# A list scheduler with new durations, a price on changes of TensorE's tiling and ScalarE's table, and new places

## The chip, the cores and the metric

The kernel runs on one core of one Trainium2 chip. A core has five engines that run their own queues of instructions: TensorE (PE in the profile, its weight loads PEld), VectorE (DVE), ScalarE (ACT), GpSimd (POOL) and SyncE (SP, which here only issues DMA transfers). The metric is the device time of one execution in microseconds (us), less is better; the median of three runs is given.

## The reference

The input `x` has 2 batches of 2048 tokens with 128 features. Four layers are added to it one after the other, each on the layer norm of its input, all in float32:

```python
x = x + attn_a(layernorm(x))    # softmax(x x^T, axis=1) x: full attention, 2048 x 2048 per batch
x = x + ffn(layernorm(x))       # two layers, see below
x = x + attn_b(layernorm(x))    # a weight per token, a weight per channel, one projection
x = x + ffn(layernorm(x))       # the same two layers and weights again

def layer(x, ...):              # one of the two layers of ffn
    h = shift_token(x)                       # half the features come from the token before
    q, k, v = split(h @ wqkv)                # 8 heads of 64
    q, k = rotary_xpos(l2norm(q) * qs, l2norm(k) * ks)
    x = x + local_attention(q, k, v) @ wo    # windows of 64, each sees itself and the one before
    h = layernorm(shift_token(x)) * lg + lb
    a, g = split(h @ w1 + b1)                # 341 each
    return x + (a * gelu(g)) @ w2 + b2
```

## The kernel before

The state is held with features on the 128 partitions (`xT`, 128 x 4096). A batch is cut into 16 blocks of 128 tokens and 4 chunks of 512.

**What one block does** (`Attention.block`, a layer's attention for 128 tokens). `project` (L584) makes queries and keys as two operations of 16 matmuls with 32 output rows each, placed in the four column strips of the array (`tile_position=(0, c * 32)`), and L591 the values with the whole array. ACT copies the values (L592) and squares the projections (L607); DVE multiplies them with the rotary tables (L608, L609) and sums the squares (L612); one whole-array matmul adds the halves (L613); ACT and POOL make the inverse root (L617, L618, `newton` L394 to L397); POOL adds the rotated halves and scales (L616, L622); DVE turns queries and keys by 32 x 32 blocks (L631, L632). `scores` (L654, with the mask added by L663) is one operation of 74 matmuls on 64 x 32 tiles. DVE takes the maximum (L675), ACT eight exponentials (L680), DVE sum and reciprocal (L686, L687), POOL scales (L692), DVE turns (L703). Four DMA writes to DRAM (L712) and one read back (L717) set the turned weights out for `combine` (L728): 32 matmuls of 64 output rows. ACT copies (L735), and every second block `out_proj` (L741) multiplies with `wo` and DVE adds it to the state (L747, L748).

**Feed-forward**, per chunk of 512: `center` (L504 to L509) makes mean and inverse root with whole-array matmuls, POOL scales (L773 in the profile), six matmul operations with `w1` (L777), of which the three gate products fill three PSUM banks until `gelus` (L785) has read them; DVE multiplies (L793), `down` (L802) multiplies with `w2`.

**Stages.** The first attention of batch 0 stands alone at the start (`first_attention`, L453 to L468). Then the program is written down tick by tick, 71 ticks: two layers of one batch run 6 ticks apart, the four passes (two batches, twice) follow each other 16 ticks apart and overlap by 7. The first attention of batch 1 (`second_attention`, L484 to L497) is spread over the first 16 ticks; its tiles `e` serve as work tiles `w` of the blocks once it is over. `token_weights` (L861 to L984) is the third layer.

**What sets the order.** None of this is the order on the engines. Each call of `op` only records an operation with its engine, a cost in us, its reads and writes, the tiles that it claims, and `late`. `Program.run` then plays the five engines forward in time with these costs: whenever an engine is free, it takes of its ready operations the one with the smallest key (its number in the program plus `late`) for which tiles are to be had, among the next `AHEAD = 600` operations. A block has some 45 operations. `TAIL` is the time from an operation's end until another engine sees it, `TABLE = 1.3` what ACT pays for another activation table (`act="E"` for exponential and logarithm, `"G"` gelu, `"S"` sigmoid). The order that comes out is the order of every queue; it is fixed when the kernel is built. Tiles come from pools (`slots`): 8 PSUM banks (`p1`), work tiles `w`, chunks `c` and others.

## Time and profile before

| | |
|---|---|
| Runs | 1557.29, 1552.46, 1549.56 us; median 1552.46 |
| Profiled execution | span 1551.6 us from first to last instruction; no time outside it is given |
| PE busy | 1456.4 us (94%), 20331 matmuls |
| DVE busy | 1337.8 us (86%) |
| POOL busy | 1071.3 us (69%) |
| ACT busy | 961.8 us (62%), of it 91.1 us in 71 table loads of 1283 ns in the table of groups, 72 in the whole trace |
| PE clock granted | 0.981 on the mean, 0.88 from 600 to 700 us, 0.86 behind 1500 us |
| DMA | 213.64 MB, engines 48.2% busy for the kernel's own queue |

PE in the profile counts a matmul from its start to its modelled end; matmuls are pipelined, so pieces of PE overlap. A 512-column product in float32 stands as two matmuls. Pieces of the chain of work that ended last give a start, a length and what worked; `x16` is the number of matmuls. A line of the waits gives who waited for whom, the total in us, how often, and the longest.

### The profile page before, as it was taken

To read this page: it belongs to the slowest core of one execution; us is meant where nothing else is said; L and a number is where in the kernel's file an instruction comes from. 1 tells how busy PE (TensorE), PEld (TensorE's weight loads), DVE (VectorE), ACT (ScalarE), POOL (GpSimd) and SP (SyncE) were. 2 spreads that over 40 slices of the span, in tenths; PEclk is the share of its full clock that TensorE was granted. 3 is DMA by queue.
4 is the path that set the end of the run, shared out by engine and by line. 5 is a ranking of instruction groups with operands and counts; after the bars stand their busy time and mean duration, and the time that the engine had idled before them with its cause. 6 is when DMAs were issued, how large, how long until landed. Compare 5 with 4: busy or idle time off the path is not lost.

```text
span 1551.6 us, 50597 instructions
## 1 busy us (share of the span) xinstructions
PE 1456.4 (94%) x20331; PEld 817.6 (53%) x20331; DVE 1337.8 (86%) x2468; ACT 961.8 (62%) x2449; POOL 1071.3 (69%) x1308
## 2 busy tenths in 40 slices
PE   7999999999999998899999999899999999999876
PEld 3455455555555554545555555545555555555443
DVE  4277866988899999979989999989999999998881
ACT  6446655666567766557656656576767676666661
POOL 4446434676598859649777869568787878895671
PEclk9999999999999999989999999899999999999998
DMA  7441442454465444535555654445646555647432
GB/s 236 147 150 45 120 113 66 117 165 117 121 167 138 139 110 113 161 106 139 154 140 141 174 135 113 105 126 161 176 136 195 161 140 164 183 139 208 125 90 71
DMA packets 204653, 213.64 MB, mean 138 GB/s; under 512 B 39594, under 2 KB 164996, under 8 KB 204420
## 3 DMA queue, kind: packets, MB, share of 16 engines
q1 hardware_dynamic: 204420, 210.43, 48.2%
q8 instruction: 160, 2.62, 0.7%
q14 instruction: 73, 0.60, 0.1%
HBM read 111.78 MB, written 61.87 MB: 112 GB/s over the span
## 4 chain that ended last, share of the span: by engine, by line
PE 56%; DVE 28%; POOL 5%; DMA 4%; issue 3%; ACT 3%; SPq 0%; POOLq 0%; DVEq 0%; ACTq 0%
PE pp L584 8%; PE pp L777 7%; PE pp L728 5%; PE pp L741 5%; PE pp L654 4%; PE pp L591 4%; PE pp L484 4%; PE pp L494 4%; PE pp L468 4%; PE pp L802 3%; DVE b_n L612 3%; DVE arena L609 2%; DVE b_m L675 2%; PE pp L460 2%; DVE b_m L686 2%
## 5 line engine op out<-in xcount | busy, mean ns | idle before, releaser
L584 PE MATMUL pp<-wqkv,b_s 128*32 128x256 f32 x4096 | 256.7, 386 | 4.8 <-DVE b_s L811 3.0
L680 ACT ACTIVATE arena<-pp,b_m 128x96 f32<-128x96 f32 x656 | 162.8, 362 | 78.3 <-DVE b_m L675 63.9
L692 POOL TENSOR_TENSOR arena<-arena,b_m 128x384 f32<-128x384 f32 x164 | 132.5, 826 | 110.6 <-DVE b_m L687 67.9
L777 PE MATMUL pp<-b_c,w 128*128 128x512 f32 (+1 forms) x384 | 181.7, 616 | 12.0 <-POOL b_c L773 8.9
L584 PEld LDWEIGHTS pp<-wqkv,b_s 128*32 128x32 f32 x4096 | 118.0, 110 | 132.6 <-issue 31.7
L607 ACT ACTIVATE arena<-pp 128x512 f32<-128x512 f32 x166 | 99.3, 618 | 82.1 <-PE pp L584 70.3
L622 POOL TENSOR_TENSOR arena<-arena,b_n 128x1024 f32<-128x1024 f32 x75 | 143.4, 1914 | 2.7
L675 DVE TENSOR_REDUCE b_m<-pp 128x4 f32<-128x384 f32 x256 | 131.0, 540 | 14.4 <-PE pp L663 13.5
L654 PEld LDWEIGHTS pp<-kring,b_c 64*32 64x32 f32 x8448 | 105.0, 106 | 70.9 <-issue 21.6
L654 PE MATMUL pp<-kring,b_c 64*32 64x96 f32 (+2 forms) x8448 | 132.8, 249 | 9.3 <-DVE kring L632 6.5
L591 PE MATMUL pp<-wqkv,b_s 128*128 128x512 f32 x256 | 138.8, 627 | 0.6 <-ACT b_c L508 0.6
L777 PEld LDWEIGHTS pp<-b_c,w 128*128 128x128 f32 (+1 forms) x384 | 66.4, 182 | 99.0 <-issue 66.0
L592 ACT COPY b_v<-pp 128x512 f32<-128x512 f32 x128 | 76.6, 599 | 58.6 <-PE pp L591 53.5
L616 POOL TENSOR_TENSOR arena<-arena 128x1024 f32<-128x1024 f32 x44 | 104.3, 2371 | 11.0 <-DVE arena L609 8.9
L616 POOL TENSOR_TENSOR right<-right,arena 128x1024 f32<-128x1024 f32 x36 | 85.2, 2368 | 34.2 <-DVE arena L609 19.8
L728 PEld LDWEIGHTS pp<-arena,b_v 128*64 128x64 f32 x2528 | 83.5, 142 | 47.1 <-issue 16.9
L728 PE MATMUL pp<-arena,b_v 128*64 128x64 f32 x2528 | 94.2, 229 | 11.6 <-DMA arena<-far 4.2
L609 DVE TENSOR_TENSOR arena<-pp,b_tab 128x512 f32<-128x512 f32 x160 | 105.0, 673 | 0.1
L680 ACT ACTIVATE right<-pp,b_m 128x96 f32<-128x96 f32 x368 | 90.8, 361 | 22.0 <-DVE b_m L675 21.5
L608 DVE TENSOR_TENSOR arena<-pp,b_tab 128x512 f32<-128x512 f32 x150 | 99.4, 674 | 4.7 <-ACT arena L607 4.0
L622 POOL TENSOR_TENSOR right<-right,b_n 128x1024 f32<-128x1024 f32 x53 | 101.3, 1913 | 2.2
L612 DVE TENSOR_REDUCE b_n<-arena 128x32 f32<-128x1024 f32 x83 | 99.3, 1199 | 0.3
(225 smaller groups left out, 3436.8 us busy)
## 6 DMA issues: line engine op xcount, KB each, us to landing
arena<-far SPq DMA_DIRECT2D x79, 512.0 KB, 4.2
b_tab<-turn SPq DMA_DIRECT2D x128, 256.0 KB, 3.5
b_v<-b_v SPq DMA_DIRECT2D x248, 128.0 KB, 3.1
far<-arena SPq DMA_DIRECT2D x312, 96.0 KB, 2.6
right<-far SPq DMA_DIRECT2D x49, 512.0 KB, 4.3
far<-right SPq DMA_DIRECT2D x200, 96.0 KB, 2.0
turn<-b_tab SPq DMA_DIRECT2D x32, 256.0 KB, 2.0
kring<-kring SPq DMA_DIRECT2D x40, 128.0 KB, 2.7
```

What stands on the lines that cost most here:

```text
L584: pe_.matmul(out=pq[k]()[c * 32 : c * 32 + 32, a * 256 : (a + 1) * 256], lhsT=s()[:, at : at + 32], rhs=wqkv[:, l, c * 256 : (c + 1) * 256 ...
L591: op("PE", 0.885, lambda: pe_.matmul(out=pv(), lhsT=h(), rhs=wqkv[:, l, 2 * INNER : 3 * INNER], start=True, stop=True), r=keys_of(s, q) + ...
L609: op("DVE", dve(512), lambda part3=part3, src=src, trig=trig: dv.tensor_tensor(part3(t2), src(), trig(1), ALU.mult), r=[pq[k], tab], w=[(t ...
L612: op("DVE", dve(1024), lambda: dv.tensor_reduce(nv()[:, 0:32], sq().rearrange("p (h d) -> p h d", d=32), AX.X, ALU.add), r=[sq], w=[nv], l ...
L616: op("POOL", pool(1024), lambda: po_.tensor_tensor(halves(t1), halves(t1), halves(t2)[:, :, ::-1, :], ALU.add), r=[t2], w=[t1], late=-51)
L622: lambda: po_.tensor_tensor(t1().rearrange("p (h d) -> p h d", d=32), t1().rearrange("p (h d) -> p h d", d=32), nr()[:, 0:32].unsqueeze(2) ...
L654: pe_.matmul(out=sim[par]()[a * 32 : a * 32 + 32, pair * 96 + c0 : pair * 96 + c0 + n], lhsT=qT()[rows, pair * P + a * 32 : pair * P + a * ...
L675: op("DVE", dve(384), lambda sim3=sim3, mx=mx: dv.tensor_reduce(mx(), sim3(), AX.X, ALU.max, negate=True), r=[sim[par]], w=[(nm, par)], la ...
L680: ac.activation(p()[:, hd * 96 : (hd + 1) * 96], sim[par]()[:, k * 96 : (k + 1) * 96], AF.Exp, bias=nm()[:, hd : hd + 1])
L692: lambda hs=hs: po_.tensor_tensor(p3()[:, hs, :], p3()[:, hs, :], rs()[:, hs].unsqueeze(2).to_broadcast([P, 4, 96]), ALU.mult),
L728: pe_.matmul(out=av()[par * 64 : par * 64 + 64, pair * P + w * WIN : pair * P + (w + 1) * WIN].rearrange("p (a c) -> p a c", a=2), lhsT=(v ...
L777: op("PE", pe(512), lambda: pe_.matmul(out=p_()[0:n, :], lhsT=w1[:, l, off + j * P : off + j * P + n], rhs=d(), start=True, stop=True), r= ...
```

## The change

No operation is added or taken away. Four things change in the planner and its figures:

- `op` takes the name of a place (`at`) and, for TensorE, a mode: `"f"` the whole array, `"p"` the projections of queries and keys, `"s"` the scores, `"v"` the weighted values. `late` is gone: a table `PLACES` gives each of some 150 places its offset, and nearly all offsets are new.
- A change of mode costs time in the plan (`SWITCH`).
- In the choice, an operation in another mode than TensorE's last one counts 25 places later (`MODE`), and an ACT operation that needs another table 300 places later (`HOLD`).
- Costs of operations are new: projections 0.97 to 0.864, scores 1.14 to 0.9, weighted values 1.13 to 0.946, output projection 1.84 to 1.74, L613 0.28 to 0.15, the eight exponentials 4 x 0.265 + 0.1 to 4 x 0.224 + 0.1 for each half, POOL's scaling 0.95 to 0.83, `act` and `pool` a little less.

Nothing else in the plan changes: pools, `AHEAD`, `TAIL` and `TABLE` stay.

```diff
+PLACES = {
+    "load1": 571, "load_x1": -350, "hybrid_kernel1": 0, "newton1": 99, "newton2": -90, "newton3": -36,
...
+    "second_attention1": 93, "second_attention2": 206, "second_attention3": -305, "second_attention4": 6,
+    "second_attention5": -143, "second_attention6": -154, "second_attention7": 846, "center1": -132, "center2": -226,
...
+    "block2": -130, "block3": -6, "block4": 254, "block5": 944, "block6": 239, "block7": 478, "block8": 417,
...
+    "block16": -133, "block17": -134, "block18": 8, "block19": 57, "block20": 479, "block21": -43, "block22": 96,
+    "block23": -331, "block24": -4, "block25": -10, "block26": -29, "block27": 4, "block28": -128, "block29": -68,
+    "block30": 221, "block31": 37, "block32": -106, "block33": 133, "block34": -102, "fold_norm1": 0,
+    "fold_norm2": 0, "fold_norm3": 0, "feed_forward1": -464, "half1": 34, "feed_forward2": 552, "feed_forward3": 41,
...
+}
...
+    MODES = "fpsv"
+    SWITCH = ((0.0, 0.231, 0.231, 0.231), (0.095, 0.0, 0.136, 0.136), (0.095, 0.136, 0.0, 0.136), (0.095, 0.136, 0.136, 0.0))
+    MODE = 25
+    HOLD = 300
...
-        o.tail, o.key = self.TAIL[eng] if tail is None else tail, o.i + late
+        o.at, o.mode = at, mode
+        o.tail, o.key = self.TAIL[eng] if tail is None else tail, o.i + PLACES[at]
...
+        def place(o):
+            if o.eng == "PE":
+                return o.key + (self.MODE if self.MODES.index(o.mode) != tiling else 0)
+            return o.key + (self.HOLD if o.act and o.act != table else 0)
...
-                ready = sorted((o for o in lines[e] if o.est <= t and o.i < begin + self.AHEAD), key=lambda o: (o.key, o.i))
+                ready = sorted((o for o in lines[e] if o.est <= t and o.i < begin + self.AHEAD), key=lambda o: (place(o), o.i))
...
+                if e == "PE":
+                    to = self.MODES.index(o.mode)
+                    end += self.SWITCH[tiling][to]
+                    tiling = to
...
-                op("PE", 0.97, lambda k=k: project(k), r=keys_of(s, q) + [wqkv_], w=[pq[k]], claim=[sq, t1, t2], late=-124)
+                op("PE", 0.864, lambda k=k: project(k), mode="p", r=keys_of(s, q) + [wqkv_], w=[pq[k]], claim=[sq, t1, t2], at="block2")
...
-            op("PE", 1.13, combine, r=[pT, v, v0], w=[av], claim=[oT], late=163)
+            op("PE", 0.946, combine, mode="v", r=[pT, v, v0], w=[av], claim=[oT], at="block30")
...
-        op("ACT", 3 * (act(512) + 0.1), gelus, r=[*pg, (b1f_, l)], w=h, act="G", late=7)
+        op("ACT", 3 * 0.58 + 0.1, gelus, r=[*pg, (b1f_, l)], w=h, act="G", at="feed_forward2")
```

Of the other places, old and new: the four writes L712 -41 and -128, the read back L717 0 and -68, the copies of the values L594 46 and 944, L598 -131 and 478, the scores' exponentials L680 -155 and -331, the squares L607 155 and 417, the output projection L741 0 and -106.

## The prediction

> **What bounds the kernel now.** I read the page's busy shares and slices first, then busy time by stretches of 100 us, then the chain of work that ended last in those stretches, then the engines' timelines and the waits.

> ```profile
> PE 1456.4 (94%) x20331; PEld 817.6 (53%) x20331; DVE 1337.8 (86%) x2468; ACT 961.8 (62%) x2449; POOL 1071.3 (69%) x1308
> ...
> PE   7999999999999998899999999899999999999876
> ...
> DVE  4277866988899999979989999989999999998881
> ```

> Two engines could be the bound: TensorE (PE) and VectorE (DVE). DVE is slack in the first third and full after it. By stretches:

> ```profile
> 200.00:300.00 100.00, 100.00 (x1170) 52.65 (x1169) 73.41 (x140) 62.65 (x163) 51.64 (x63) 1.00 0.37 101
> ...
> 400.00:500.00 100.00, 99.42 (x1533) 57.21 (x1531) 91.26 (x163) 63.02 (x158) 77.39 (x94) 1.00 0.53 141
> ...
> 1300.00:1400.00 100.00, 94.44 (x1698) 55.07 (x1686) 99.49 (x183) 66.89 (x181) 87.84 (x106) 1.00 0.58 165
> ```

> Columns are length, then busy us (and count) of PE, weight loads, DVE, ACT, POOL. Up to 500 us PE hardly stops while DVE waits; after that, to 1500 us, DVE is at 85 to 99 and PE at 87 to 99. Between its instructions, counted in the trace, DVE idles 53 us before 100 us, 71 to 500, 55 to 1500 and 30 behind; PE 13, 1, 64 and 14. The chain agrees: summed over its pieces, PE has 480 of the first 500 us; of 500 to 1500 us it has 380, DVE 410, POOL 85, DMA 54, the rest ACT and issue.

> What a change of TensorE's tiling costs stands in the chain's pieces (start, us, what). L584 is the projection in column tiles (mode p), L654 the scores (s), L728 the weighted values (v); the others use the whole array (f).

> ```profile
> 390.70 1.00 PE pp L584 x16
> 391.70 0.86 PE pp L654 x53
> ...
> 392.75 0.34 PE pp L613 x2
> ...
> 425.27 0.14 PE pp L613 x2
> ...
> 455.31 3.59 PE pp L584 x64
> ```

> One projection alone (x16) takes 1.00, four in a row (x64) 3.59. So one is (3.59 - 1.00) / 3 = 0.863 and a tiled stretch pays 0.137 besides. A whole-array product between two tiled ones pays too: L613 takes 0.34 there and 0.14 among its like, 0.20 more. An excursion from f to a tiled mode and back is thus 0.33, a change between two tiled modes 0.137. The new table of switches says 0.231 + 0.095 and 0.136: it agrees.

> Counted in the trace's order of PE instructions there are 670 stretches of one mode: 273 of f, 157 of p (for 256 projections; 82 stand alone), 120 each of s and v (for 128 each). That is 272 excursions and 125 changes inside them: 272 x 0.33 + 125 x 0.137 = 107 us of PE, 26 of it before 500 us (164 of the changes).

> ScalarE's tables, in its timeline:

> ```profile
> 807.78 0.23 ACT L617 ACTIVATE b_n<-b_n 128x32 f32<-128x32 f32 x1
> 808.03 1.28 ACT L241 ACT_TABLE_LOAD   x1
> 809.32 1.83 ACT L785 ACTIVATE b_c<-pp,b1f 128x512 f32<-128x512 f32 x3
> 811.17 1.28 ACT L241 ACT_TABLE_LOAD   x1
> ```

> A load is 1.28 and stops ACT for nothing more. There are 72: nearly two for each of the 32 gelu steps.

> **The change, part by part.** No instruction of the computation is added or removed; only their order on each queue changes, and the number of table loads. All numbers below are against the profiled execution's span of 1551.6, which lies 0.9 under the median of the three runs (1552.46); the page shows no time outside it.

> *Switches counted and a tiled neighbour preferred (MODE = 25).* An operation in another mode than PE's is put 25 places back. The second projection of a block is made one place after the first, so with the bonus it follows at once unless its PSUM bank is not free: I take all pairs as closed, 157 to 128 stretches, 29 fewer. For s and v the choice is thin. The norm's product starts a median 0.7 us after its sum is done and the output projection 1.6 us after its copy, so about one PE operation queues at a time; 25 places are about half of one block's operations. I take one in eight of the 240 stretches as joined, 30 fewer. Each tiled stretch costs 107 / 397 = 0.27, so 59 x 0.27 = 16 us of PE. On the path is what lies before 500 us (26 of 107) and 38% of the rest: (26 + 0.38 x 81) / 107 = 0.53, so 8.5 us. Bounds: two blocks always sharing one excursion, 64 x 0.33 + 128 x 0.137 = 39, saves 68, on the path 36; every tiled operation alone, 512 x 0.33 = 169, costs 62, on the path 33. I take 8.5, nearer the first row of a thin queue. When PE gets faster after 500 us, DVE is late next: it idles only 55 of those 1000 us, which caps all gains there.

> *Places of the second batch's first attention.* Its score products go from 0 to 93 places back, its exponentials from -103 to +206, its adds from 70 to 846. Lines 484 and 494 hold 61.3 + 58.1 us of PE before 500 us, just where PE is full and DVE idles 71 us (100 to 500). Work moved behind lets the blocks' DVE work come earlier. I take a fifth of the 71: 14 us. Bounds: 71 gained; or a loss of one tick (1551.6 / 71 ticks = 22 us), because the exponentials' tiles become work tiles of the blocks only when the attention is over.

> *The other places and the durations.* Old costs held the switches as an average (a projection 0.97 where the row says 0.863; scores 1.14, now 0.9), so the old line was planned with waits in wrong spots. After 500 us DVE idles 55 and PE 64. I take a fifth of DVE's 55: 11 us. Bounds: all 55 gained, or as much lost, since a plan that fits the chip badly can add as many waits as there are now. POOL and SP get new places too (the four writes of the turned weights go from -41 to -128, their read back from 0 to -68, the copies of v from 46 to 944): on SP's queue a write that waits for its transpose holds up the table loads and v copies behind it. The rows for that are the PE waits on these landings, which are small now:

> ```profile
> PE pp L728 <- DMA right<-far: 5.8, 5, 2.5
> ...
> PE pp L728 <- DMA arena<-far: 4.2, 5, 1.5
> ```

> *Tables (HOLD = 300).* Fewer loads save 1.28 each on an engine that is busy 62% and has 3% of the chain: nothing on the path, at most a few us. The price is that a gelu waits until no other ready operation of ACT is nearer than 300 places. I take nothing for it, since ACT idles 38% of the time and a ready gelu is then taken at once; without that cover it costs what the slower rival below counts, 63.

> Sum: 8.5 + 14 + 11 = 33.5 less: 1518 against the span, 1519 against the median.

> [...]

> **The rivals.** *Larger gain.* The search finds orders in which two blocks share most excursions, and the balance of the first third is found: 25 + 35 + 25 = 85 less, 1467. For it: 107 us of switches that the old planner could not see. Against: the thin queue, and DVE's 1337.8 busy with 53 us of start and 30 of tail in which it has nothing to do: 1421 is a floor.

> *No difference.* The queue is so thin that the stretches stay above 640 and the new places only reshuffle the waits: 1545 to 1560. For it: PE operations start about one operation after they are released. Against: the 82 lone projections, whose pairs are ready together.

> *Slower: the gelus come too late.* Their place goes from 7 to 552 and the hold adds 300. Until a gelu step has run it keeps three of the eight PSUM banks (its three gate products), and PE then stands for want of banks; DVE's product behind it stood 12.5 us in three waits. If each of the 32 waits for one more group of eight exponentials (L680 x8: 1.97), and none of it is hidden, that is 63; less the 33.5 that is 1581. It decides from 33.5 / 32 = 1.05 us on the path per gelu step. Against: the planner knows the banks and pays for such a wait in its own plan.

> **How the numbers follow.** The case summed above 0.57, with its own range 1485 to 1544 (twice the sum, or its first term alone); the larger gain 0.12; no difference 0.09; slower 0.22. A measurement of this kernel can tell about 0.5% (8 us) from no change. Faster is 0.57 + 0.12 = 0.69, same 0.09, slower 0.22. The range takes in the larger gain and most of the slower case: 1468 to 1578 leaves about 0.06 below and 0.10 above.

> **What would show it.** In the changed trace: at most 610 stretches of one mode, projections almost all in pairs (L584 x32 or longer in the chain); less DVE idle between 100 and 500 us than 71; L484 and L494 reaching further right; at most 72 table loads; PE's pieces in the chain without waits in the first third. It is wrong if the stretches do not fall, if ACT's gelu (L785) or DVE's product (L793) gathers waits of many us and PE waits for banks behind them, or if PE's waits for landings (L728) grow from today's 10 us to tens.

## The result and the profile after

Over 16 runs each the changed kernel takes 1556.12 us (1550.54 to 1564.95) and the kernel before 1549.77 us (1543.95 to 1559.08): a ratio of 1.0042 [1.0022, 1.0063]. That is within the 0.5% that I call no difference, a hair on the slow side. I had forecast 1519.

The page of the changed kernel (lines 630, 700, 709, 774, 823 and 831 are the old 584, 654, 663, 728, 777 and 785):

```profile
PE 1460.6 (94%) x20331; PEld 825.7 (53%) x20331; DVE 1343.1 (86%) x2468; ACT 962.3 (62%) x2450; POOL 1073.8 (69%) x1308
...
PE   7999999999999999789999999999998999989976
...
DVE  4367868888999999899999999899998999998871
...
PEclk9999999999999999799999999899999999999997
...
q8 instruction: 160, 2.62, 0.7%
...
PE 49%; DVE 32%; POOL 7%; issue 5%; DMA 3%; ACT 3%; SPq 1%; POOLq 0%; DVEq 0%; ACTq 0%
```

From the page of the kernel before, to set beside them:

```profile
PEclk9999999999999999989999999899999999999998
...
q8 instruction: 160, 2.62, 0.7%
...
PE 56%; DVE 28%; POOL 5%; DMA 4%; issue 3%; ACT 3%; SPq 0%; POOLq 0%; DVEq 0%; ACTq 0%
```

Every engine is as busy as before to 6 us. In the chain TensorE's share is lower and "issue" higher, 5% against 3%: time in which an engine stands and nothing that the profile shows holds it. Busy time by stretches, after and then before; behind the length stand busy us (and count) of PE, weight loads, DVE, ACT and POOL, then the granted clock, the DMA share and GB/s:

```profile
100.00:500.00 400.00, 395.81 (x5126) 219.19 (x5124) 336.46 (x628) 247.24 (x655) 258.47 (x307) 1.00 0.44 125
500.00:1000.00 500.00, 469.61 (x6989) 270.05 (x6988) 477.55 (x866) 320.38 (x798) 379.43 (x472) 0.96 0.48 134
1000.00:1400.00 400.00, 378.72 (x6322) 215.69 (x6307) 382.43 (x689) 266.31 (x698) 319.22 (x380) 0.98 0.56 157
1400.00:1550.00 150.00, 126.82 (x1636) 74.33 (x1634) 99.73 (x175) 74.94 (x173) 75.72 (x91) 0.89 0.41 112
```

```profile
100.00:500.00 400.00, 398.39 (x4984) 215.26 (x4982) 329.11 (x611) 249.44 (x650) 252.21 (x304) 1.00 0.43 120
500.00:1000.00 500.00, 462.02 (x7011) 264.26 (x7012) 474.53 (x865) 313.38 (x790) 373.23 (x452) 0.96 0.49 133
1000.00:1400.00 400.00, 386.61 (x6418) 222.00 (x6414) 384.78 (x697) 268.40 (x697) 326.09 (x400) 0.99 0.56 159
1400.00:1550.00 150.00, 120.98 (x1640) 70.16 (x1638) 102.51 (x184) 79.12 (x190) 77.10 (x93) 0.95 0.44 121
```

Up to 500 us the changed kernel gets more done: 142 more matmuls and 7.4 us more of DVE. Between 860 and 1165 us its output projections end 7 to 21 us ahead of the old ones, 12 in the median (ends of the n-th one, counted in both traces); from 1165 to 1400 it is 1 to 12, 6 in the median, and at the end nothing. The third row shows the giving back: 96 fewer matmuls. The last shows the clock: 0.89 against 0.95.

Two things that eat into the lead show in the chain. The first is a stop in the scores, in its pieces (start, us, what):

```profile
1159.42 5.42 PE pp L823 x12
...
1166.91 0.68 PE pp L700 x50
1167.59 3.27 issue
1170.86 0.38 PE pp L700 x3
```

After a row of 50 products in the scores TensorE stands 3.27 us; then the last products follow. No other engine is waited for. The second comes behind a stand of TensorE: the granted clock falls to 0.50. The product L823, 5.42 us for twelve matmuls in the first row, takes 7.57 us for ten 210 us later, behind a wait of 3.74 us for POOL; there the granted clock is 0.50 from 1368.7 to 1375.5 us:

```profile
1369.41 7.57 PE pp L823 x10
```

I call time x (1 - granted clock), summed over the clock's records, the clock loss: 45.6 us after, 30.4 before. The profiled pair is typical. Over its 16 runs the changed kernel's mean clock is 0.970, a loss of 47 us; over 53 runs of the kernel before, made beside the experiments, it is 0.977 to 0.979, 32 to 35 us. The scatter from run to run goes with the clock too: over 20 runs of the kernel before, span and clock correlate with -0.84, 12 us for each 0.01.

The stops, in the waits (who waited for whom: us in total, times, longest):

```profile
PE pp L823 <- POOL b_c L819: 10.9, 10, 3.7
PE pp L700 <- issue: 10.7, 6, 3.3
...
PE pp L774 <- DMA right<-far: 5.5, 2, 3.5
```

Before:

```profile
PE pp L654 <- issue: 1.8, 3, 0.9
```

### The profile page after: what moved, and what is told of

The parts are those of the page before. It is cut to its first block, busy times and chain, and to the rows that moved or that the text cites. A ratio compares the mean times of both kernels' runs of the same rounds, so it can differ in the third digit from the quotient of the medians.

```text
span 1553.4 us, 50570 instructions
## 1 busy us (share of the span) xinstructions
PE 1460.6 (94%) x20331; PEld 825.7 (53%) x20331; DVE 1343.1 (86%) x2468; ACT 962.3 (62%) x2450; POOL 1073.8 (69%) x1308
## 4 chain that ended last, share of the span: by engine, by line
PE 49%; DVE 32%; POOL 7%; issue 5%; DMA 3%; ACT 3%; SPq 1%; POOLq 0%; DVEq 0%; ACTq 0%
PE pp L630 7%; PE pp L823 7%; PE pp L774 4%; PE pp L540 4%; PE pp L514 4%; PE pp L700 3%; PE pp L787 3%; PE pp L637 3%; PE pp L530 3%; DVE b_n L658 3%; PE pp L848 3%; DVE b_m L721 3%; DVE arena L655 2%; DVE b_m L732 2%; PE pp L506 2%
## 5 line engine op out<-in xcount | busy, mean ns | idle before, releaser
L738 POOL TENSOR_TENSOR arena<-arena,b_m 128x384 f32<-128x384 f32 x172 | 139.3, 830 | 104.0 <-DVE b_m L733 56.5
L726 ACT ACTIVATE arena<-pp,b_m 128x96 f32<-128x96 f32 x688 | 170.0, 366 | 60.8 <-DVE b_m L721 55.9
L823 PE MATMUL pp<-b_c,w 128*128 128x512 f32 (+1 forms) x384 | 189.7, 637 | 11.8 <-POOL b_c L819 10.9
L668 POOL TENSOR_TENSOR arena<-arena,b_n 128x1024 f32<-128x1024 f32 x77 | 147.2, 1914 | 2.8
L700 PE MATMUL pp<-kring,b_c 64*32 64x96 f32 (+2 forms) x8448 | 131.4, 248 | 14.8 <-issue 10.7
L721 DVE TENSOR_REDUCE b_m<-pp 128x4 f32<-128x384 f32 x256 | 130.6, 539 | 14.0 <-PE pp L709 13.1
L662 POOL TENSOR_TENSOR arena<-arena 128x1024 f32<-128x1024 f32 x48 | 113.6, 2368 | 35.8 <-DVE arena L654 31.7
L653 ACT ACTIVATE arena<-pp 128x512 f32<-128x512 f32 x148 | 89.1, 618 | 60.1 <-PE pp L630 58.1
L823 PEld LDWEIGHTS pp<-b_c,w 128*128 128x128 f32 (+1 forms) x384 | 68.9, 189 | 98.3 <-issue 68.8
L655 DVE TENSOR_TENSOR arena<-pp,b_tab 128x512 f32<-128x512 f32 x166 | 108.8, 672 | 4.5 <-ACT right L653 2.4
L726 ACT ACTIVATE right<-pp,b_m 128x96 f32<-128x96 f32 x336 | 83.6, 368 | 38.9 <-DVE b_m L721 27.0
L654 DVE TENSOR_TENSOR arena<-pp,b_tab 128x512 f32<-128x512 f32 x154 | 100.9, 671 | 0.1
L668 POOL TENSOR_TENSOR right<-right,b_n 128x1024 f32<-128x1024 f32 x51 | 97.6, 1915 | 2.1
L848 PE MATMUL pp<-b_c,w 128*128 128x512 f32 (+1 forms) x192 | 90.4, 606 | 0.0
```

What stands on the lines that cost most here:

```text
L655: op("DVE", dve(512), lambda part3=part3, src=src, trig=trig: dv.tensor_tensor(part3(t2), src(), trig(1), ALU.mult), r=[pq[k], tab], w=[(t ...
L662: op("POOL", pool(1024), lambda: po_.tensor_tensor(halves(t1), halves(t1), halves(t2)[:, :, ::-1, :], ALU.add), r=[t2], w=[t1], at="block14")
L668: lambda: po_.tensor_tensor(t1().rearrange("p (h d) -> p h d", d=32), t1().rearrange("p (h d) -> p h d", d=32), nr()[:, 0:32].unsqueeze(2) ...
L700: pe_.matmul(out=sim[par]()[a * 32 : a * 32 + 32, pair * 96 + c0 : pair * 96 + c0 + n], lhsT=qT()[rows, pair * P + a * 32 : pair * P + a * ...
L721: op("DVE", dve(384), lambda sim3=sim3, mx=mx: dv.tensor_reduce(mx(), sim3(), AX.X, ALU.max, negate=True), r=[sim[par]], w=[(nm, par)], at ...
L726: ac.activation(p()[:, hd * 96 : (hd + 1) * 96], sim[par]()[:, k * 96 : (k + 1) * 96], AF.Exp, bias=nm()[:, hd : hd + 1])
```

## Experiments

The planner gives its own end time when it has fixed the order: 1538.3 us for the kernel before (with its old costs), 1510.9 for the changed one (with its new costs). On the chip the one is some 15 us over its plan, the other 44. So the question was why a plan that is 27 us shorter brings no shorter time on the chip.

### e1: no two scores in a row

With switches priced, 16 scores operations follow another scores operation directly (8 before), and 8.6 of the 11.2 us of stops inside TensorE's operations lay in 4 of these 16. The edit moves the second one behind the next operation where nothing forbids it:

```diff
+            if a.mode == b.mode == "s" and x.mode != "s" and b not in x.deps and x.t0 - b.t1 < 0.1:
+                order.remove(b)
+                order.insert(order.index(x) + 1, b)
```

> The changed kernel with 12 of its 16 scores operations that follow a scores operation moved one place back on PE, behind the next operation of another mode; nothing else moves. Theory 'bursts': two scores operations in a row use up TensorE's instructions faster than they arrive, and the stops inside scores operations (10.7 us in the changed kernel, 8.6 of it in scores that follow scores) fall under 4 us; about 4 us of tiling switches come back (12 x 0.33), so it is 4 to 8 us faster than the changed kernel: about 1549 to 1552, ratio to before 0.997 to 1.002. Rival 'hidden': those stops lie beside DVE's work, the stops go but the time stays at 1554 to 1558 (ratio 1.003 to 1.007).

Measured: 1561.29 us, ratio 1.0046 [1.0022, 1.007] to the kernel before: the changed kernel's own ratio. Stops in scores that follow scores fell to 1.7 us, but those in the other scores rose from 2.1 to 7.9; the sum inside operations went only from 11.2 to 10.3. Moving the neighbours moves the stops.

### e2: TensorE kept busy in its waits

65 filler matmuls (128 x 256, into the bank that the waiting operation overwrites) go ahead of 30 TensorE operations that waited over 0.8 us in the changed kernel's trace:

```diff
+            for _ in range(WARM.get(o.i, 0)):
+                warm(o.bank())
             o.fn()
...
+    g.run(tc, slots, turn, lambda bank: pe_.matmul(out=bank[:, 0:256], lhsT=meanw, rhs=wqkv[:, 0, 0:256], start=True, stop=True))
```

> The changed kernel with 65 extra whole-array products (128 x 256, results overwritten) in front of the 30 PE operations that waited over 0.8 us for another engine, filling some 60% of each wait; order of everything else unchanged. Theory 'clock': a PE wait of 2 us and more costs half clock afterwards, 91 us at half clock = 45.6 us lost in the changed kernel against 30.4 before; with the waits filled the half-clock time falls under 50 us and the kernel gets 8 to 18 us faster than the changed one (1538 to 1548, ratio 0.992 to 0.999). Rival 'marker': the half clock falls where PE has nothing to do, the clock gets better but the time stays within 3 us of the changed kernel, or the extra 28 us of PE make it longer (1555 to 1565).

Measured: 1544.12 us, ratio 0.9929 [0.9907, 0.9951], 1.1% less than the changed kernel's ratio. The clock loss fell from 45.6 to 22.0 us. The page of this kernel:

```profile
PE 1474.2 (95%) x20461; PEld 841.5 (54%) x20461; DVE 1340.6 (87%) x2468; ACT 962.3 (62%) x2450; POOL 1073.1 (69%) x1308
...
PEclk9999999999999999889999999899999999999999
```

TensorE has 14 us more work and the kernel is faster: the clock is a real cost here, not an accompaniment. Not all of the gain need be the clock's: the stops over 0.8 us that no semaphore ends fell too, from 10.7 to 5.5 us. The clean case is e7 below, where they stay (1.9 and 2.1 us).

### e3 and e4: the planner's other settings

`MODE = 100` in place of 25, and the changed planner with the old places.

> The changed kernel with the preference for TensorE's mode at 100 places instead of 25, places not searched again. The order has 568 stretches of one mode instead of 637 and 89.0 us of switches instead of 100.3; the planner's own end is 1541.6 instead of 1510.9. Theory 'plan': chip time is the plan's end plus the changed kernel's slip of 44: 1586. Theory 'fitted places': the slip of 44 came with places that were searched for the shortest plan; an order that was not searched slips as the one before (15): 1557. Theory 'bursts': more scores follow scores and the stops inside scores operations exceed 15 us.

Measured: 1584.96 us, ratio 1.0187 [1.0152, 1.0223]. It has 568 stretches of one mode, 69 fewer than the changed kernel, and is slower.

> The changed kernel with the places of the kernel before: new durations, prices and preferences alone. 629 stretches of one mode, 99.1 us of switches, planner's own end 1552.1. Theory 'plan': 1552 + 44 = 1596. Theory 'fitted places': 1552 + 15 = 1567. If it is at 1550 or under, preferring a mode is a gain by itself and the new places took it back.

Measured: 1600.89 us, ratio 1.0292 [1.0257, 1.0326]. Both lie within 5 us of where "plan + 44 us" put them, although e4's places were not searched against the new costs at all. So the 44 us are not the price of a search that has gone too far.

### e5 and e6: is it the shorter costs of ScalarE and GpSimd?

The kernel before, the changed one, e3 and e4 fitted another reading: the old costs of ACT and POOL, 77 and 44 us longer in sum, had left the plan an allowance. Walked through with TensorE's new costs and these old ones, the four orders end only 7 to 10 us under their spans (the expectation below counts 4 to 9). e5 puts them back (the two below, the gelus, and the formulas `act` and `pool`) and searches the places anew:

```diff
-                op("ACT", 4 * 0.224 + 0.1, weights, r=[sim[par], (nm, par)], w=[(p, par)], act="E", at="block23")
+                op("ACT", 4 * 0.265 + 0.1, weights, r=[sim[par], (nm, par)], w=[(p, par)], act="E", at="block23")
...
-                    "POOL", 0.83,
+                    "POOL", 0.95,
```

> The changed scheduler with TensorE's new costs, switches and MODE kept, ScalarE's and GpSimd's costs put back to what they were before the change, and the places searched anew against this plan (some 25,000 plans, starting from the old places). Its plan ends at 1523.0; the same order walked through with all of the new costs ends at 1516.9; 611 mode stretches. Theory 'the new ScalarE and GpSimd costs took out the plan's allowance': the plan with the old ones stands 4 to 9 us under the chip, as it did for the four kernels measured (before 1542 to 1550, after 1547 to 1556), so 1527 to 1532 us, about 1.6% faster than the changed kernel. Rival 'any plan that a search has driven down loses some 44 us on the chip': 1516.9 + 44 = 1561.

Measured: 1549.56 us, ratio 0.9963 [0.9939, 0.9987]: faster than both kernels by a little, but 17 us and more above the theory and 11 under its rival.

e6 gives the kernel before the new places and nothing else.

> The kernel before with the new places and nothing else: old costs, no MODE, no switches. Its plan (old costs) ends at 1548.1, 664 mode stretches. Walked through with TensorE's new costs and the old ones of ScalarE and GpSimd its order ends at 1550.1: by the theory 1554 to 1559 us, 0.3 to 0.6% slower than before. Rival 'new costs plus 44': 1540.4 + 44 = 1584, 2% slower.

Measured: 1573.16 us, ratio 1.0107 [1.0079, 1.0135]; again between the two. The allowance theory falls: it fitted the four kernels from which it was made and neither of the next two.

### What the slip is made of

I then walked each kernel's fixed order through with the changed kernel's costs, and once more with what its own trace shows of TensorE: first the half-clock loss inside its operations, then the stops inside them as well. The two middle columns give by how much the end moves, to some 3 us: how a loss is shared out over the operations is a choice. In us:

| kernel | new costs | + half clock | + stops | all three | span on the chip |
|---|---|---|---|---|---|
| before | 1533.7 | 19.4 | 4.1 | 1557.2 | 1551.6 |
| after | 1510.2 | 30.4 | 9.9 | 1550.5 | 1553.4 |
| e1 | 1517.9 | 23.3 | 8.3 | 1549.5 | 1554.0 |
| e3 | 1541.1 | 35.4 | 8.7 | 1585.2 | 1583.4 |
| e4 | 1551.7 | 35.5 | 3.6 | 1590.8 | 1595.8 |
| e5 | 1516.9 | 26.2 | 7.6 | 1550.7 | 1551.1 |
| e6 | 1540.4 | 28.5 | 8.2 | 1577.1 | 1572.6 |
| e8 (below) | 1510.4 | 24.6 | 13.1 | 1548.1 | 1556.0 |

The last two columns agree within 8 us for eight orders whose spans differ by up to 45. Between before and after: the order is 23.5 us shorter by the costs; half clock takes 11.0 of it and the stops 5.8; 8.5 stay unexplained (the walk is 5.6 over the chip before and 2.9 under it after); 1.8 are left the wrong way. The half clock itself comes with waits (it followed all 17 full-clock windows of 3.41 us in which TensorE was busy for under 41%, see the last section), so this is bookkeeping, and the fillers are the test of cause.

### e7 and e10: fillers in other orders

> The kernel before with 75 filler matmuls of 128x256 ahead of the 38 TensorE operations that waited over 0.8 us in its trace (the outputs stay the same). In the changed kernel 65 of them took the clock loss from 45.6 to 22.0 us and the time down by 12. Theory 'the clock falls after waits in any order of this work': before's loss goes from 30.4 to about 20 us and the time down by 4 to 8 us, 1542 to 1548. Rival 'the fillers helped only because the changed order leaves more long waits': no change, or slower by the fillers that start late, 1550 to 1558.

Measured: 1546.39 us, ratio 0.9939 [0.9916, 0.9963]; clock loss from 30.4 to 13.5 us. Its page:

```profile
PE 1476.5 (96%) x20481; PEld 837.5 (54%) x20481; DVE 1336.3 (86%) x2468; ACT 962.8 (62%) x2449; POOL 1072.4 (69%) x1308
```

So the kernel before gains as well, about half of what the changed one gains from its fillers (0.6% against 1.1%), and with fillers both stand at one ratio, 0.993 and 0.994. With much of the clock loss gone the two orders still are of one speed. That does not make the clock blameless: e2 still loses 8.5 us more of it than e7 (22.0 against 13.5) and 3 us more in stops. But the 23.5 us of the plan do not appear.

> The kernel of e5_own_costs (old costs on ScalarE and GpSimd, places searched for them) with 83 filler matmuls of 128x256 ahead of the 34 TensorE operations that waited over 0.8 us in its trace (outputs the same). Its clock loss was 37.3 us. Theory 'half of the clock loss comes back as time, in any order': loss down to about 20 us, 8 to 12 us faster than e5_own_costs, a ratio of 0.988 to 0.991 to the kernel before, and with it the fastest kernel of this study. Rival 'the fillers help only where a plan leaves long waits of its own': the ratio stays at 0.996.

Measured: 1535.1 us (1534.29 to 1537.37), ratio 0.9888 [0.983, 0.9946]; clock loss from 37.3 to 10.3 us. It is the fastest kernel here, 1.1% under the kernel before and 1.5% under the changed one by the ratios. Here too the stops fell with the clock loss, from 9.8 to 2.5 us, so that the two are not told apart. Its page:

```profile
PE 1470.7 (96%) x20497; PEld 840.6 (55%) x20497; DVE 1336.7 (87%) x2468; ACT 962.3 (63%) x2450; POOL 1073.0 (70%) x1308
...
DVE  4357877889899999999999999999999999998782
...
PEclk9999999999999999899999999999999999999999
...
PE 66%; DVE 21%; DMA 4%; POOL 3%; issue 3%; ACT 1%; SPq 1%; POOLq 0%; DVEq 0%; ACTq 0%
```

Only one slice of the clock is below 0.9, and VectorE has 25 slices in a row at 0.9 or more; in the changed kernel the longest such row is 8.

### e8: planning for the two terms

If the clock and the stops can be modelled, the places should be searched against them.

> The changed kernel with other places and nothing else. They were searched by the plan's order walked through with two terms that the plan lacks: TensorE at half clock for the 3.41 us after any stretch of 3.41 us in which it is busy for less than 55%, and a stop of 1.8 us ahead of 8% of the scores operations. Planned end 1511.1 against 1510.9 of the changed kernel, 650 mode stretches against 637; with the two terms 1539.5 against 1547.2, modelled clock loss 20.7 against 25.2 us. Theory 'the two missing terms make the difference': 8 us faster than the changed kernel, 1546 to 1551 us. Rival 'the slip comes from elsewhere and is the same for each plan of this kind': 1511.1 + 44 = 1555. Rival 'stretches decide': 13 more of them, 2 us slower than the changed kernel, 1558.

Measured: 1558.63 us, ratio 1.004 [1.0018, 1.0063], as the changed kernel. The clock loss did come down (37.4 us in the profile, 40 over ten runs, against 45.6 and 47), but the stops went from 9.9 to 13.1 us (in the table) and other waits grew. The theory's sum is wrong though one of its terms is right: what explains the times afterwards could not be planned with, at least not in this crude form.

### e9: what the stops are

> The kernel before with each of the 128 scores operations carried out twice in a row (the outputs stay the same). A second one is 66 more matmuls with their loads straight after the first 66, with no other work between. One look at what TensorE stops for in the second half. Theory 'instructions run short in back-to-back scores': 0.5 us a second half, as in the 16 scores that follow scores in the changed kernel (8.6 us), so 60 to 70 us of stops without a releaser and some 107 + 65 us more time. Rival 'the stops are not from scores following scores': under 10 us of stops, and some 107 us or less more time.

```diff
-            op("PE", 1.26 if first else 1.14, scores, r=...
+            op("PE", 1.26 if first else 1.14, lambda: (scores(), scores()), r=...
```

Measured, in one run: 1761.93 us, 209 more than the kernel before (1553.09). The waits of this kernel:

```profile
PE pp L654 <- issue: 65.7, 43, 3.4
PE pp L663 <- issue: 12.4, 8, 2.4
```

and in its page

```profile
PE 1597.8 (91%) x29803; PEld 939.7 (53%) x29803; DVE 1346.7 (77%) x2468; ACT 966.6 (55%) x2449; POOL 1072.7 (61%) x1308
...
q8 instruction: 234, 3.83, 1.0%
```

TensorE has 141 us more work and 78 us of stops in scores and mask. The theory gave 60 to 70 of stops and 172 more time, the rival under 10 and 107. Then I counted TensorE's instructions from stop to stop: products, weight loads and the semaphore waits between them. The distances between the 47 stops over 0.8 us that no semaphore ends are multiples of 256, each of them exactly: 768, 256, 2816, 2048, 6144, 1024, 1024, 512 and so on. In the changed kernel, with six such stops in the scores, they are 10240, 256, 7936, 10496, 3840; in the kernel before, with two, 18176, which is 71 x 256. So in each of the three kernels these stops lie on a grid of 256 instructions. The page's instruction queue fits: its packets are 3.83 MB / 234 = 16.4 KB, 64 bytes each for 256 instructions, and e9's 74 additional packets (160 before) hold its 18944 additional instructions (18944 / 256 = 74). The packets' times settle it: each of these 55 stops ends 1.1 to 1.6 us after a packet of this queue has landed. My reading is that TensorE stood there for the next 256 instructions. Of the three tiled modes scores use 256 instructions up fastest, estimated from their counts and times: mostly 144 instructions (72 products and their loads; the 74 given above is the mean, with 104 in 8 of the 128) in some 0.85 us from first to last start, so 256 in 1.5 us; a projection takes 32 in 0.86, so 256 in 6.9 us.

Most packets come without such a stop in the changed kernel: against the 160 of this queue stand six stops over 0.8 us in the scores. In e9 it is 47 stops against 234 packets, at 0.8 us to 3.4 us each.

## Why the prediction was wrong

**The third term failed, and with it the forecast.** "The other places and the durations" counted a truer plan as worth 11 us, with a loss of as much as 55 as the far bound. The plan did get 23.5 us shorter in its own terms, but DVE's idle time from 500 to 1500 us is 56.6 us against 55: nothing was gained there. The step in it that failed was "so the old line was planned with waits in wrong spots". The old costs were wrong in size, but the old order has less half clock than any other in the table, and fewer stops than all but e4. Neither stands in either planner, and the prediction has no term for them: it took TensorE's clock and its stops as unchanged without saying so, and by the table they cost the new order 11.0 and 5.8 us of its 23.5. e4 (new planner, old places: +2.9%) and e6 (old planner, new places: +1.1%) show that places fit only the planner for which they were searched; the pair moves the time by 0.4%.

**The first term was mis-sized.** Forecast: 59 fewer tiled stretches, 16 us of PE, 8.5 on the path. Counted: 380 tiled ones against 397, 17 fewer, and with those of the whole array 637 against 670; priced by the planner's own table of switches 100.3 against 105.7 us, 5.4 us of PE. "I take all pairs as closed" was wrong: projections make 154 stretches, not 128, and 87 stand alone, 5 more than before. The other joins were 14, not 30. And TensorE's busy time rose by 4.2 us all the same: it worked 77 us at half clock, against 52 before. Nor do stretches decide the time: 568 in e3, 1.9% slower; 611 in e5, 0.4% faster.

**The second term was right in kind.** DVE's idle time from 100 to 500 us fell from 71 to 63.5 us, half of the 14 that I took, and the lead stood at some 12 us from 860 to 1165 us. It was given back after that, where I had taken a lead once won as kept.

**Tables: worth nothing, as forecast.** There are 73 loads against 72, one more than the "at most 72" that I had set as a sign. With `HOLD` at 0 the planner writes the identical order, so that part of the change does nothing.

**The rivals.** What came is "no difference", in its range of 1545 to 1560 and in part by its mechanism, a queue too thin for a preference of 25 places to bite (637 stretches; I had written above 640). With 100 places it bites, 568 in e3, but the plan is then 31 us longer. The half clock and the stops are not in that rival either, so that its number came out right is partly luck. Its chance of 0.09 was too low: its counter, the 82 lone projections "whose pairs are ready together", was read from the program's order, not from the trace. The slower rival did not come: in the changed kernel's waits TensorE waits nowhere for the gelu (L831), and DVE's product waits 12.1 us in one wait, against 12.5 in three. PE's waits for landings at the weighted values did not grow: 8.7 us against 10.0. That TensorE has no room, on which the prediction's first term rests, stands: with 141 us more of PE and 78 us of stops e9 took 209 longer, so nearly all of it was paid.

Open is why the old order has less half clock than the new ones, and the 8.5 us of the table that no term holds. The table is bookkeeping after the event, to 8 us an order; what the runs show as causes is that filled waits bring back clock and time (e7: the clock loss from 30.4 to 13.5 us, the time down by 0.6%), and that the stops go with the packets of instructions, with TensorE going on 1.1 to 1.6 us after one has landed (e9).

## What to carry to other kernels

A planner's shorter end is worth only what its missing terms leave: before believing a re-fitted cost model, walk old and new order through the same costs and compare the gap to the chip for both. An offset that fits four kernels is not yet a law; the fifth and sixth run were worth more than the fit. Where TensorE is the bound and waits a few us here and there, filler matmuls in the waits brought 0.6 to 1.1%, in the three orders tried.
